# ScalarE issues the stores of the dense groups, SyncE their landings and loads, and each segment's rows are scaled one group sooner

## Chip, cores and metric

One core of a Trainium2 chip. The metric is the device time of one execution in microseconds; beside it stands one execution under the profiler, with its span from the first to the last instruction of the kernel. Engines are named as in the profile: PE (matmul), DVE (VectorE), ACT (ScalarE), POOL (GpSimd), SP (SyncE).

## What is computed

N = 16384 tokens of 256 features, each with a segment number `bids` from 0 to 7. Tokens are placed in padded segments of 3072 rows, attended within their segment, projected, normalized over all tokens and added to the input:

```python
q, k, v = feat @ Wq, feat @ Wk, feat @ Wv
starts = jnp.searchsorted(bids, jnp.arange(B))
pos = jnp.arange(N) - starts[bids]
qp, kp, vp = pad(q), pad(k), pad(v)
scores = jnp.where(mask[:, None, :], einsum(qp, kp), NEG)
r = einsum(softmax(scores), vp)[bids, pos]
t = r @ Wt
tn = (t - t.mean(0)) / jnp.sqrt(t.var(0) + EPS) * gamma + beta
return feat + jax.nn.relu(tn)
```

`bids` is not sorted. So only tokens whose `pos` lies within 3072 of zero own a row of their segment; all others read one of two edge rows of a segment.

## The kernel before

`fast_path` writes each engine's program once, in the order in which operations are added with `pg.op`; `Program.settle` works out from the boxes that an operation reads and writes which semaphores it must wait for. Each engine runs its own list in that order, so an operation that waits holds all that stand behind it on its engine.

First come eight segments of attention, up to 6 tiles of 128 rows each. Their rows lie in `tk` (line 939), the gathered inputs in `xs`. The table `order` (line 989), a list of the 16 dense groups, is computed early on DVE; SP reads its 16 entries into registers (line 1531, through `load`, line 1068: one register load and two register instructions behind it). POOL likewise reads `upto`, the count of groups that each segment needs.

Then follows the last stage. Sums over all tokens give mean and variance; the chain on DVE goes through a square root on ACT (line 1860) to `scale` and `shift`, and to the 16 edge rows in three bf16 parts (`y3`). The dense groups (loop at line 1933, NG = 16) each write 1024 tokens of the output, all as if they were edge readers: group k's input is loaded into buffer `fb[k % NF]` (NF = 10, `load_group`, line 1698), PE multiplies a one-hot table `hot` with `y3` into four PSUM banks (24 matmuls), and the sum of input and banks goes back to `fb`. `PAIRS` (line 1872) says for how many of the four banks PE also adds the input (`open_group`) so that ACT only copies the bank (line 1949); the others DVE adds (line 1952, "addition k" below). The banks of even and odd groups alternate, so PE's group k+2 needs the banks that addition k and copy k free.

All 17 stores (`store`, line 1923; group 0 in two halves) are issued by SP. After store k SP waits for the landing of store k-1 and raises `groups_done` (`finish`, line 1920), then issues load k-3+NF (line 1957). From k = 3 to 10 DVE scales, shifts and adds the rows of segment k-3 behind addition k (`normal`, line 1892: three operations over four tiles; `normal_more`, line 1904: three more for a fifth and a sixth tile, if the segment has them), at k = 11 the 3 tiles of late rows `tl`. POOL scatters these rows over the output (lines 1981 to 1998), for each segment only after enough groups have landed: the wait at line 1982. At the end each engine loads a flag and looks at it (`look`, line 1970); the landing of store 15 is waited for by SP behind its look (line 1979).

Of the kernel before, what the change touches and what calls it, by code (L numbers as in the profile page):

```python
# [21 lines left out]
NB = 8  # L22
# [878 lines left out]
def fast_path(nc, feat, bids, wq, wk, wv, wt, gamma, beta, out, bad):  # L901
# [6 lines left out]
    NG = J // GT  # L908
# [3 lines left out]
    pg = Fast(nc)  # L912
# [12 lines left out]
    def new(name, shape, dtype=F32):  # L925
        nonlocal end
        size = mybir.dt.size(dtype)
        for d in shape[1:]:
            size *= d
        plan.append((name, shape, dtype, end))  # L930
        h = at(name, shape, dtype, end)
        end += size + -size % 32
        return h
# [8 lines left out]
    vs, q, k = [None] * 2, [None] * 2, [None] * 2  # L942
# [17 lines left out]
    NF = len(fb)  # L960
# [28 lines left out]
    upto, order = new("upto", [1, NB + 1], I32), new("order", [1, NG], I32)  # L989
# [76 lines left out]
    regs = pg.sized  # L1066

    def load(eng, key, ap, hi, lo=0):
        def emit(e):
            regs[key] = e.value_load(ap, min_val=lo, max_val=hi)  # L1070

        pg.op(eng, emit, [ap], [], bare=True)
# [623 lines left out]
    GR = GT * P  # L1696

    def load_group(k):
        f = fb[k % NF]

        def emit(e):
            rows = feat[ds(regs[("order", k)] * GR, GR), :]
            return e.dma_start(f[:], rows.rearrange("(p i) d -> p i d", p=P))

        pg.op("SP", emit, [], [f[:]], dma=True)
# [129 lines left out]

    for g in range(MID, NF):
        load_group(g)
    for t in range(LT):
        pg.gather(tl[:, t, :], t_rows, ridl[:, t : t + 1], NB * FW)

# [33 lines left out]
    def open_group(k):  # L1874
        f = fb[k % NF]
        for r in range(4 - PAIRS[k], 4):
            pg.mm(
                bank[4 * ((k + 1) % 2) + r][:], ident[:], f[:, 2 * r : 2 * r + 2, :].rearrange("p t d -> p (t d)"),
                start=True, stop=False,
            )  # L1880
# [11 lines left out]
    def normal(m, T, y=tk, x=xs):  # L1892
        y, x = y[:, m : m + T, :], x[:, m : m + T, :]

        def over_t(a):
            return a.unsqueeze(1).to_broadcast([P, T, D])

        pg.tt(y, y, over_t(scale), ALU.mult)
        pg.tt(y, y, over_t(shift), ALU.add)
        pg.stt(y, y, 0.0, x, ALU.max, ALU.add)  # L1900
# [3 lines left out]
    def normal_more(e, t):  # L1904
        m = e * FT + t
        y, x, sem, n = tk[:, m, :], xs[:, m, :], row_done[e], 3 * (t - 4)

        def emit(v):
            with v.If(regs[("td", e)] > t - 4):
                v.tensor_tensor(y, y, scale, ALU.mult).then_inc(sem, 1)  # L1910
                v.wait_ge(sem, n + 1)
                v.tensor_tensor(y, y, shift, ALU.add).then_inc(sem, 1)  # L1912
                v.wait_ge(sem, n + 2)
                v.scalar_tensor_tensor(y, y, 0.0, x, ALU.max, ALU.add).then_inc(sem, 1)

        pg.op("DVE", emit, [y, x, ss[:]], [])
# [3 lines left out]
    def finish(w):  # L1920
        pg.op("SP", lambda e: e.sem_inc(done, 1), [], [], after=w)

    def store(k, lo, hi):
        f = fb[k % NF]

        def emit(e):
            rows = out[ds(regs[("order", k)] * GR, GR), :]
            return e.dma_start(rows.rearrange("(p i) d -> p i d", p=P)[:, lo:hi, :], f[:, lo:hi, :])

        return pg.op("SP", emit, [f[:, lo:hi, :]], [], dma=True)  # L1930

    stores = []
    for k in range(NG):
        f = fb[k % NF]
        b0 = 4 * ((k + 1) % 2)
        own_pairs = 4 - PAIRS[k]
        if k >= 2:
            open_group(k)
        for u in range(2):
            for part in range(3):  # L1940
                for r in range(4):
                    s = slice(32 * r, 32 * r + 2 * NB)
                    pg.mm(
                        bank[b0 + r][:, u * D : (u + 1) * D], hot[s, k, u, :], y3[part][s, :],
                        start=(r < own_pairs and part == 0), stop=(part == 2),
                    )
        if own_pairs < 4:
            rows = f[:, 2 * own_pairs : 8, :].rearrange("p t d -> p (t d)")
            pg.copy("ACT", rows, psum[:, b0 + own_pairs : b0 + 4, :].rearrange("p b d -> p (b d)"))
        for lo, hi in ((0, 2), (2, 3)) if k == 0 else ((0, own_pairs),):  # L1950
            rows = f[:, 2 * lo : 2 * hi, :].rearrange("p t d -> p (t d)")
            added = pg.tt(rows, rows, psum[:, b0 + lo : b0 + hi, :].rearrange("p b d -> p (b d)"), ALU.add)
        stores.append([store(k, 0, 4), store(k, 4, 8)] if k == 0 else [store(k, 0, 8)])
        if k >= 1:
            finish(stores[k - 1])
        if k >= 3 and k - 3 + NF < NG:
            load_group(k - 3 + NF)
        if 3 <= k < 3 + NB:
            e = k - 3
            normal(e * FT, 4)  # L1960
            normal_more(e, 4)
            normal_more(e, 5)
        if k == 3 + NB:
            normal(0, LT, tl, xl)
    again = {}

    for eng in ENGINES:
# [2 lines left out]
    def look(eng, after=()):  # L1970
        def emit(e):
            again[eng] = (e, regs[("again", eng)], e.mark_branch_hint_location())

        pg.op(eng, emit, [], [], bare=True, after=after)

    look("PE", [added])
    for eng in ("ACT", "DVE", "SP"):
        look(eng)
    finish(stores[NG - 1])

    for e in range(NB):
        pg.op("POOL", lambda x, e=e: (x.wait_ge(done, 1), x.wait_ge(done, regs[("g", e)])), [], [])
# [26 lines left out]
def whole(nc, feat, bids, wq, wk, wv, wt, gamma, beta, out):  # L2009
    with nc.sbuf_tensor("bad", [P, 1], I32) as bad:  # L2010
        ends = fast_path(nc, feat, bids, wq, wk, wv, wt, gamma, beta, out, bad)
        engines = [e for e, _, _ in ends]
        for e, again, mark in ends:
            e.br_cond(again > 0, "general", "all_done").branch_hint(mark)
        with nc.body("general", valid_engines=OrderedEngineSet([e.engine for e in engines])):
            nc.all_engine_barrier()
            with tile.TileContext(nc) as tc:
                any_lengths(tc, feat, bids, wq, wk, wv, wt, gamma, beta, out)
        nc.switch_bb("all_done")
# [34 lines left out]
```

## Time and profile before

| | us |
|---|---|
| median of 3 runs (lowest to highest) | 341.26 (341.05 to 342.02) |
| profiled execution, its own time | 340.02 |
| its span | 335.6 |
| DVE busy in the span | 238.0 (71%) |
| PE busy | 258.8 (77%) |
| POOL busy | 135.4 (40%) |
| ACT busy | 151.4 (45%) |
| last Square on ACT, and the Sqrt after it | 235.91, 242.90 |
| dense groups: first addition, last addition ends | 248.25, 329.1 |
| mean DMA rate from 254 to 302 | about 395 GB/s |

The profile counts from the first instruction. A row of a timeline gives start, duration, engine, line, operation, output<-input, and in brackets how long the engine was idle before it and what ended that. "remote" or "another core or an unknown queue" means that the profile has no instruction that matches the end of the wait. Busy time of PE and POOL is rough: PE's ends are modelled, and POOL's spans are approximate. The DMA queue q1 is SP's, q10 ACT's, q0 POOL's.

### The profile page before, as it was taken

The numbers are of one execution on the slowest core, as the hardware profiler recorded it, in microseconds if no ns is written. First come the engines' busy times: TensorE is split into PE (matmuls) and PEld (weight loads), VectorE is DVE, ScalarE is ACT, GpSimd is POOL, SyncE is SP. The second block draws the span as 40 slices with busy tenths as digits, with TensorE's granted clock in tenths as the row PEclk, the third lists the DMA queues.
The fourth block names the chain that finished last, engine by engine and source line by source line (L and its number), as shares of the span: only waits on it lengthen the run. The fifth ranks groups of instructions, "written<-read, shape, count | busy, mean of one in ns | idle before, by whom it ended". The sixth has DMA issues, their size and how long they took to land.

```text
span 335.6 us, 4870 instructions
## 1 busy us (share of the span) xinstructions
PE 258.8 (77%) x1407; PEld 169.9 (51%) x1407; DVE 238.0 (71%) x765; ACT 151.4 (45%) x294; POOL 135.4 (40%) x143
## 2 busy tenths in 40 slices
PE   5699799998998999899999979295858966455100
PEld 2466556666666777677667856164423422122000
DVE  4835679996775759478759878445589999999202
ACT  3126968767755762656476377384310311110000
POOL 6434215060350160325003647742120647887750
PEclk9999989999999999999999999769585976555555
DMA  3101004151171033203001210399969999997933
GB/s 99 33 22 47 17 3 130 41 152 37 29 169 48 0 88 115 66 9 109 31 3 47 83 32 2 114 375 389 418 267 373 315 428 420 422 413 294 373 115 131
DMA packets 21533, 52.50 MB, mean 156 GB/s; under 512 B 5488, under 2 KB 14786, under 8 KB 17530
## 3 DMA queue, kind: packets, MB, share of 16 engines
q1 hardware_dynamic: 15674, 41.37, 32.4%
q0 software_dynamic: 5280, 10.18, 10.2%
q10 hardware_dynamic: 544, 0.52, 0.5%
q8 instruction: 16, 0.26, 0.3%
q14 instruction: 19, 0.16, 0.1%
HBM read 26.27 MB, written 28.74 MB: 164 GB/s over the span
## 4 chain that ended last, share of the span: by engine, by line
PE 45%; DVE 25%; ACT 9%; issue 6%; another core or an unknown queue 6%; POOL 3%; DMA 2%; POOLq 0%; DVEq 0%
PE ps L802 43%; DVE f L821 7%; DVE tk L821 5%; ACT pa L812 4%; ACT xT L812 2%; PE ps L807 2%; DMA ecat<-t_rows,eidx 2%; ACT vs L817 2%; DVE junk L828 1%; DVE k L818 1%; POOL sel L830 1%; DVE tk L1910 1%; DVE tk L1912 1%; DVE w L821 1%
## 5 line engine op out<-in xcount | busy, mean ns | idle before, releaser
L877 POOL DMA_INDIRECT xs<-in_r_feat,idx x48 | 51.0, 1063 | 118.9 <-DVE idx L841 70.3
L802 PE MATMUL ps<-vs,pa 128*128 128x257 f32 x312 | 80.7, 404 | 10.5 <-ACT tk L812 6.0
L802 PEld LDWEIGHTS ps<-vs,pa 128*128 128x128 f32 x312 | 59.1, 198 | 24.9 <-issue 10.3
L893 POOL DMA_INDIRECT out<-tk,idx x32 | 36.6, 1144 | 28.0 <-DVE f L821 15.8
L802 PE MATMUL ps<-wvt,xT 128*128 128x256 f32 x156 | 37.4, 386 | 0.7 <-ACT vs L817 0.7
L817 ACT COPY f<-ps 128x1024 f32<-128x1024 f32 (+1 forms) x12 | 10.0, 834 | 61.4 <-remote 40.2
L802 PE MATMUL ps<-y,hot 16*128 16x256 bf16 x384 | 20.1, 356 | 22.5 <-DVE f L821 14.5
L821 DVE TENSOR_TENSOR f<-f,ps 128x1024 f32<-128x1024 f32 (+3 forms) x17 | 26.2, 1561 | 14.9 <-remote 14.2
L802 PEld LDWEIGHTS ps<-wvt,xT 128*128 128x128 f32 x156 | 28.8, 190 | 11.0 <-ACT sq L812 2.3
L812 ACT ACTIVATE pa<-ps,mask 128x512 f32<-128x512 f32 x48 | 29.5, 687 | 10.2 <-PE ps L802 9.8
L802 PEld LDWEIGHTS ps<-y,hot 16*128 16x128 bf16 x384 | 11.0, 117 | 40.3 <-DVE f L821 21.3
L802 PE MATMUL ps<-f,ident 128*128 128x512 f32 x38 | 27.7, 854 | 1.6 <-DVE f L821 0.9
L854 DVE RECIPROCAL rdens<-ps 128x1 f32<-128x1 f32 x48 | 7.7, 160 | 27.3 <-PE ps L802 23.9
L817 ACT COPY vs<-ps 128x512 f32<-128x512 f32 x24 | 14.1, 589 | 27.1 <-PE ps L802 17.3
L812 ACT ACTIVATE xT<-ps,negx 128x512 f32<-128x512 f32 (+1 forms) x32 | 16.9, 581 | 19.4 <-PE ps L807 9.8
L818 DVE COPY k<-ps 32x128 f32<-32x128 f32 x48 | 14.1, 294 | 16.0 <-PE ps L802 13.3
L802 PE MATMUL ps<-xT,w 128*128 128x512 f32 (+1 forms) x48 | 22.0, 586 | 1.5 <-ACT xT L812 1.5
L812 ACT ACTIVATE q<-ps,cqk 96x512 f32<-96x512 f32 (+3 forms) x32 | 18.3, 573 | 10.3 <-PE ps L802 10.0
L841 DVE SCALAR_TENSOR_TENSOR acc<-tk,reads_r,acc 128x256 f32<-128x256 f32 x45 | 21.4, 476 | 2.0 <-issue 1.3
L841 DVE SCALAR_TENSOR_TENSOR acc<-sq,reads_r,acc 128x256 f32<-128x256 f32 x45 | 21.7, 483 | 0.0
L812 ACT ACTIVATE pb<-ps,mask 128x256 f32<-128x256 f32 x48 | 19.2, 475 | 4.1 <-PE ps L802 3.8
L802 PE MATMUL ps<-q,k 32*128 32x512 f32 (+1 forms) x124 | 20.0, 560 | 0.0
(264 smaller groups left out, 420.9 us busy)
## 6 DMA issues: line engine op xcount, KB each, us to landing
f<-in_r_feat SPq DMA_DIRECT2D x16, 1024.0 KB, 9.8
out<-f SPq DMA_DIRECT2D x15, 1024.0 KB
t_rows<-tk SPq DMA_DIRECT2D x8, 512.0 KB, 5.8
t_rows<-tk SPq DMA_DIRECT2D x8, 256.0 KB, 3.3
eb<-edge_of SPq DMA_DIRECT2D x16, 64.0 KB
out<-f SPq DMA_DIRECT2D x2, 512.0 KB, 3.4
xs<-in_r_feat,idx POOLq DMA_INDIRECT x48, 3.1
out<-tk,idx POOLq DMA_INDIRECT x39
```

The costliest lines, as they stand in the source:

```text
L802: "PE", lambda e: e.matmul(out, lhsT, rhs, start=start, stop=stop, skip_group_check=True),
L807: return self.op("PE", lambda e: e.transpose(out, in_, ident), [in_, ident], [out], pred=pred)
L812: "ACT", lambda e: e.activation(out, in_, func, bias=bias, scale=scale), [in_, *more], [out]
L817: return self.op("ACT", lambda e: e.copy(out, in_), [in_], [out])
L818: return self.op(eng, lambda e: e.tensor_copy(out, in_), [in_], [out])
L821: return self.op(eng, lambda e: e.tensor_tensor(out, a, b, op), [a, b], [out])
L828: lambda e: e.tensor_scalar(out, a, s1, s2, op0, op1, accum_out=accum)
L830: else e.tensor_scalar(out, a, s1, s2, op0, op1),
L841: else e.scalar_tensor_tensor(out, a, s, b, op0, op1),
L854: return self.op("DVE", lambda e: e.reciprocal(out, in_), [in_], [out])
L877: lambda e: e.indirect_dma_start(out=out, out_offset=None, in_=table, in_offset=bass.IndirectOffsetOnAxis(ap=ind, axis=0), bounds_check=n ...
L893: lambda e: e.indirect_dma_start(out=table, out_offset=bass.IndirectOffsetOnAxis(ap=ind, axis=0), in_=src, in_offset=None, bounds_check=n ...
```

## The change

Four things change. ACT reads the 16 entries of `order` into registers of its own (key "at"), in its order behind the last operation of the attention and ahead of the square root. The stores are issued by ACT. The store of group k-1 is put behind ACT's copy of group k, and `finish` of that store and the load that it makes room for follow at once on SP, so loads come as soon as the store that frees their buffer has landed, instead of three groups later. And the rows of segment e are scaled behind addition e+2 instead of e+3; `tl` behind addition 10. The wait for the last landing moves ahead of SP's flag load and look.

```diff
     for g in range(MID, NF):
         load_group(g)
+    for k in range(NG):
+        load("ACT", ("at", k), order[0:1, k : k + 1], NG - 1)
     for t in range(LT):
         pg.gather(tl[:, t, :], t_rows, ridl[:, t : t + 1], NB * FW)
...
         def emit(e):
-            rows = out[ds(regs[("order", k)] * GR, GR), :]
+            rows = out[ds(regs[("at", k)] * GR, GR), :]
             return e.dma_start(rows.rearrange("(p i) d -> p i d", p=P)[:, lo:hi, :], f[:, lo:hi, :])
 
-        return pg.op("SP", emit, [f[:, lo:hi, :]], [], dma=True)
+        return pg.op("ACT", emit, [f[:, lo:hi, :]], [], dma=True)
 
     stores = []
+
+    def send(k):
+        stores.append([store(k, 0, 4), store(k, 4, 8)] if k == 0 else [store(k, 0, 8)])
+        finish(stores[k])
+        if k + NF < NG:
+            load_group(k + NF)
+
     for k in range(NG):
...
             pg.copy("ACT", rows, psum[:, b0 + own_pairs : b0 + 4, :].rearrange("p b d -> p (b d)"))
+        if k >= 1:
+            send(k - 1)
         for lo, hi in ((0, 2), (2, 3)) if k == 0 else ((0, own_pairs),):
...
-        stores.append([store(k, 0, 4), store(k, 4, 8)] if k == 0 else [store(k, 0, 8)])
-        if k >= 1:
-            finish(stores[k - 1])
-        if k >= 3 and k - 3 + NF < NG:
-            load_group(k - 3 + NF)
-        if 3 <= k < 3 + NB:
-            e = k - 3
+        if 2 <= k < 2 + NB:
+            e = k - 2
             normal(e * FT, 4)
             normal_more(e, 4)
             normal_more(e, 5)
-        if k == 3 + NB:
+        if k == 2 + NB:
             normal(0, LT, tl, xl)
+    send(NG - 1)
     again = {}
...
     for eng in ("ACT", "DVE", "SP"):
         look(eng)
-    finish(stores[NG - 1])
```

## The prediction

> **What bounds the kernel now.** I read the busy table in slices first: from about 246 us the kernel is in its last stage, the dense groups, where DVE and the DMA engines are both full. Then the chain of waits of the end:
>
> ```profile
> 306.88 1.24 DVE f L821
> 308.12 0.42 issue
> 308.55 2.28 DVE f L821
> 310.82 3.16 another core or an unknown queue
> 314.00 0.04 issue
> 314.04 1.75 DVE f L821
> 315.79 10.90 another core or an unknown queue
> 326.75 0.04 issue
> 326.79 2.29 DVE f L821
> ```
>
> The last two additions of a group (k=14, k=15) wait 3.16 and 10.90 us for something the page can't name. It isn't the load: the landing records in the trace put the last load at 298.4. What is left is PE's bank for that group, whose matmuls the trace draws as ended at 312.4. After the last addition (329.1) the store of group 15 is issued, lands at 334.8 (SP's landing record, line 1921), and the span ends at 335.6. The table by stretches shows the stage before it:
>
> ```profile
> 278.00:286.00 8.00, 5.10 (x28) 1.95 (x28) 7.80 (x12) 1.01 (x1) 6.47 (x6) 0.58 1.02 424
> 286.00:294.00 8.00, 3.51 (x30) 1.31 (x34) 7.79 (x12) 1.01 (x1) 6.17 (x7) 0.50 1.02 420
> ...
> 318.00:326.00 8.00, 0.00 (x0) 0.00 (x0) 0.00 (x0) 0.00 (x0) 5.02 (x6) 0.50 0.44 159
> ```
>
> Columns: length, busy time of PE, PE loads, DVE, ACT, POOL, clock, DMA share, GB/s. DVE is 97% busy and DMA full; at 318 to 326 POOL alone works. So I read POOL's timeline:
>
> ```profile
> 261.30 1.71 POOL L893 DMA_INDIRECT out<-tk,idx  x1 [15.17 <-DVE f L821]
> ...
> 265.91 1.83 POOL L893 DMA_INDIRECT out<-tk,idx  x1 [0.30 <-DVE f L821]
> 271.45 0.98 POOL L893 DMA_INDIRECT out<-tk,idx  x1 [3.71 <-SPq L1921]
> ```
>
> POOL's scatters of segment 1 wait for SP's landing count, not for rows: by lines 1453 to 1481 and the inputs, segments 0 to 7 need 3, 5, 5, 7, 7, 7, 11 and 11 landed groups, and the fifth landing was counted at 270.6. The rows of segment 1 were ready at 264.6. From 271.45 on POOL issues one scatter every 1.29 us or slower, without a pause, to 324.54; its drain (L789) ends at 331.9, three microseconds before the last store. POOL's chain is the second bound, close behind the first.
>
> **What the Trainium skill says.** "DMA: Bandwidth & Descriptors", section "Issuing engines are not separate DMA queues": DMAs from scalar, sync and gpsimd run on the same 16 engines, and several issuers only save issue time. The trace agrees on the size of that: 17 stores at 0.33 us of SP each, while the DMA share stands at 1.02. The same page, "Queues, rings and completion order": each DMA engine goes round-robin between the rows that have work, packet by packet. In the kernel before, stores and loads sit in one row (q1) in issue order, so its trace doesn't show it. "Perfetto Trace Analysis", "Summary: the profiler window per engine type": TensorE's end is estimated. This trace fits: drawn end 312.4, addition released at 326.75.
>
> **The change, part by part.** The profiled execution took 340.02, its span 335.6; the median of the runs is 341.26, 1.24 above it. I sum against 335.6.
>
> 1. *Sixteen register loads on ACT.* They stand in ACT's order after the last Square and ahead of the Sqrt for the scale, on which all of DVE's later work hangs:
>
> ```profile
> 235.91 0.42 ACT L812 ACTIVATE sq<-tk 128x256 f32<-128x256 f32 x1
> 236.34 1.28 ACT L812 ACT_TABLE_LOAD   x1
> 242.90 0.30 ACT L812 ACTIVATE s<-v,eps_t 128x8 f32<-128x8 f32 x1 [5.27 <-DVE v L830]
> ```
>
> SP does the same sixteen, and ACT has one load at its end (line 1070):
>
> ```profile
> L1070 SPq TENSOR_LOAD <-order x16: 265/267/489, 79.3 to 87.8; - x16
> ...
> L1070 ACTq TENSOR_LOAD <-bad x1: 1067/1067/1067, 314.1 to 314.1; - x1
> ```
>
> Each load has two register instructions behind it: on SP sixteen took 79.3 to 88.4 = 9.0 us. Started at 235.95 they end at 244.95, 2.05 past 242.90. If the table load stays next to its Sqrt, behind them, 1.28 more: D = 3.4. Lower end: 2.1, the table load ahead. Upper end: ACT's only load in the trace took 1.6 with what follows it; sixteen of those are 25.8, D = 20. That one was a first load, and SP's and POOL's first were also slower than their next (0.49 against 0.27), so I take D = 3.6, a slow first one included. Nothing hides it: DVE waits at 242.9 for the Sqrt, and PE and the loads of the first ten groups (landed by 249.6) are early.
>
> 2. *Stores from ACT.* SP loses 17 issues of 0.33, and nobody waited for them. ACT gains 17 of some 0.48 (its two issues at the start: 0.465 and 0.497). The store of k-1 waits for DVE's addition k-1 and holds what is behind it on ACT: the copy of k+1. That copy needs PE's banks of k+1, which the same addition frees, and PE takes 0.8 us or more after that: covered, so 0; without the cover 0.5 a group. The store of k-1 also waits for the copy of k, normally done earlier; for k=14 (copy at 314.06, addition 13 done 310.83) it leaves 3.2 late, covered by the store of 15 being last.
>
> 3. *Loads on SP at once after a landing.* Loads 10 to 15 were issued at 260.6, 263.4, 270.8, 276.4, 282.9, 288.7 and each landed 13 us or more before its first reader (load 10 at 266.9, PE's matmul with group 10 at 280.5; load 14 at 290.4, PE at 305.5): no gain from having them sooner. But they now share the engines with the stores from another row, instead of standing behind stores 0 to 3. This is the hidden cost, taken in 5.
>
> 4. *Rows one group sooner.* DVE's sum is the same, 98% full to 310.8; only the order moves. Additions 3 to 10 come later by one segment's rows (3.7 us for four tiles, up to 6.2 with two more). Addition 4 ended at 260.97; now additions 0 to 2 (254.0), rows 0 (3.7), addition 3 (2.3), rows 1 (3.7), addition 4 (1.2): 264.85 + D = 268.4. The rows were not what POOL waited for, so the earlier rows gain nothing, and the fifth landing gets later.
>
> 5. *POOL's start.* Before: store 4 issued 261.2, landed 270.6, behind one load. After: issued 268.5. If the engines gave it all, it would land 3.4 later (the median landing of the half store): 271.9. With loads taking half from about 258.5: stores have moved 1.8 of 5.24 MB by then (0.37 MB/us, as in this stretch before), the other 3.4 go at 0.185: 277. I take 277, between 271.9 and 279. POOL's segment 1 starts near 277.5 instead of 271.45: +6 (range +1.4 to +8). All its later gates (landing 7 near 288, landing 11 near 310, rows) are met before it gets there, so its 53.1 us follow unchanged, ending at 330.6.
>
> 6. *The last landing on SP.* The wait for landing 15 now stands ahead of SP's load of the flag, which was done while the store was under way (329.54 to 330.44). It comes after the landing now: +0.95 on the path to the end.
>
> **Sum.** DVE and store tail: D 3.6 + 0.95 = +4.5, if the 10.90 wait stays. If that wait goes with POOL's last scatter (326.7 against 324.54), 6 + 0.95 = +7. POOL's own end: 331.9 + 6 + 0.7 = 338.6, +3.0. I take +4.7, since the first needs only that the wait stays what it is: 340.02 + 4.7 + 1.24 = **346.0**; this case's own range is 344.8 to 348.6.
>
> **Rivals.**
> - *The tail wait goes away, POOL ends the kernel* (slower side, 0.20). For it: loads are out of the way at the end. Additions 14 and 15 then end at 318.8, the last store by 328, and the end is POOL's 338.6: 344.3, or 342 with a POOL start at +4.
> - *The same, with a short POOL shift: faster* (0.14). If stores aren't slowed by loads, store 4 lands at 271.9, POOL shifts by 1.4 and ends at 331.9 + 1.4 + 0.7 = 334.0, 1.6 under 335.6: 339.7. It decides where POOL's start is under 2.9 later and the 10.90 wait is gone. Against it: the wait follows PE's last group, which the diff leaves as it is.
> - *Within 0.3%* (0.08): the two effects meet, 340.2 to 342.3.
> - *ACT's loads at its own 1.6 each* (0.04): D near 20, about 362.
> - The main case has 0.54. That the change doesn't do what it says I rule out: the store's queue is in the diff.
>
> A measurement of this kernel can tell about 0.3% from no change. Faster 0.14, same 0.08, slower 0.78. The range leaves out the faster rival's lower part and the 1.6 us loads: 339.8 to 350.
>
> **What would show it.** Right: sixteen TENSOR_LOADs on ACT from about 236, the Sqrt at 246.3 to 246.6 instead of 242.90; stores on q10; addition 4 ending near 268.4; landing 5 counted near 277 and POOL's segment 1 released by it; loads 10 to 15 issued by 284; a flag load on SP after the last landing. Wrong: a Sqrt still near 243 (step 1), landing 5 at or before 271 (step 5), or the last addition following addition 13 without a wait, which would take the main case with it.

## The result and the profile after

| | before | after |
|---|---|---|
| median of the runs, same job | 341.64 (341.05 to 342.56) | 352.56 (351.95 to 353.85) |
| profiled execution, its span | 340.02, 335.6 | 353.07, 348.5 |
| Sqrt on ACT starts | 242.90 | 246.70 |
| addition 4 ends | 260.97 | 268.66 |
| fifth landing counted | 270.6 | 279.5 |
| last scatter issued | 323.56 | 331.53 |
| last landing counted | 334.8 | 346.8 |

The ratio is 1.0322, 95% interval 1.0281 to 1.0363: slower by 10.9 us, where 4.7 was forecast; 352.56 lies outside the range of 339.8 to 350. A job is one set of kernels measured together on one chip, the kernel before among them. Comparisons below are made within one job unless the text says otherwise, because the kernel before itself took 330 in some jobs and 339 to 342 in others; how these jobs differ is told with the experiments. A ratio compares only those runs of a kernel that lie within 1.5% of its fastest; a median is of all runs.

The chain of waits of the changed kernel, its end (start, length, what it was):

```profile
309.26 1.75 DVE f L821
311.06 1.61 PE ps L802 x24
312.73 1.75 DVE f L821
314.48 15.31 another core or an unknown queue
329.88 2.29 DVE f L821
332.17 3.46 another core or an unknown queue
335.69 0.85 DVE f L821
...
337.49 2.15 DVE f L821
```

Before, the two unexplained waits were 3.16 and 10.90 us and stood ahead of additions 14 and 15. Now they are 15.31 and 3.46 and stand ahead of additions 13 and 14. One group was left behind the long wait; now there are three, and their stores are issued within 4 us of one another, at 335.87, 337.61 and 339.81.

The queues show the change itself. The stores' 16.78 MB have moved from q1 to q10, where 0.52 MB of ACT's own stood before. First before, then after:

```profile
q1 hardware_dynamic: 15674, 41.37, 32.4%
q10 hardware_dynamic: 544, 0.52, 0.5%
...
q1 hardware_dynamic: 13226, 24.60, 19.2%
q10 hardware_dynamic: 2992, 17.30, 12.3%
```

ACT's timeline after, around the Sqrt and around stores 3 and 4 (start, length, idle time before in brackets):

```profile
235.57 0.42 ACT L812 ACTIVATE sq<-tk 128x256 f32<-128x256 f32 x1
245.41 1.28 ACT L812 ACT_TABLE_LOAD   x1 [9.42 <-issue]
246.70 0.30 ACT L812 ACTIVATE s<-v,eps_t 128x8 f32<-128x8 f32 x1
...
264.04 0.34 ACTq L1930 DMA_DIRECT2D out<-f  x1
269.59 1.01 ACT L817 COPY f<-ps 128x1024 f32<-128x1024 f32 x1 [5.13 <-PE ps L802]
269.81 0.34 ACTq L1930 DMA_DIRECT2D out<-f  x1
```

The 9.42 us of "issue" are the sixteen register loads; the table load stands behind them. Store 4 goes out at 269.81, although its addition ended at 268.66: copy 5, which stands ahead of it on ACT, waited for PE.

POOL's timeline after:

```profile
265.62 1.55 POOL L893 DMA_INDIRECT out<-tk,idx  x1 [20.37 <-DVE tk L821]
...
280.37 0.98 POOL L893 DMA_INDIRECT out<-tk,idx  x1 [8.43 <-SPq L1923]
...
331.53 0.98 POOL L893 DMA_INDIRECT out<-tl,idx  x1 [0.30 <-issue]
```

Segment 1 again waits for SP's count of landings, now for 8.43 us, and starts 8.9 later than before.

PE's timeline after shows what the chain can't name:

```profile
306.88 1.47 PE L802 MATMUL ps<-y,hot 16*128 16x256 bf16 x24
311.06 1.47 PE L802 MATMUL ps<-y,hot 16*128 16x256 bf16 x24 [2.70 <-DVE f L821]
...
317.00 0.38 PE L802 MATMUL ps<-y,hot 16*128 16x256 bf16 x1 [0.34 <-issue]
318.41 0.41 PE L802 MATMUL ps<-y,hot 16*128 16x256 bf16 x2 [1.03 <-issue]
319.84 0.43 PE L802 MATMUL ps<-y,hot 16*128 16x256 bf16 x3 [1.01 <-issue]
```

Group 13's 24 matmuls are drawn from 311.06 as if they took 1.47 us, but group 14's weight loads and matmuls then enter in steps of 0.71 us (in the single records 316.99, 317.71, 318.41, 319.14, 319.84), as they would behind work that goes at that pace. PE's semaphore, on which the additions wait, tells the real ends: group 12 done at 312.67, group 13 at 329.79, 0.09 us ahead of addition 13. That is 17.1 us, or 24 x 0.71. I call this the crawl. Before, PE's semaphore for group 15 came at 326.70, 14.4 us after its drawn end: the same thing, one group at the end. The pace isn't the same everywhere: before, group 15 was done 12.7 us after group 14, which is 0.53 us for each matmul.

### The profile page after: what moved, and what is told of

Same layout as the page of the kernel before. It is cut to its first block, busy times and chain, and to the rows that moved or that the text cites. A ratio compares the mean times of both kernels' runs of the same rounds, so it can differ in the third digit from the quotient of the medians.

```text
span 348.5 us, 4934 instructions
## 1 busy us (share of the span) xinstructions
PE 264.0 (76%) x1407; PEld 170.1 (49%) x1407; DVE 237.9 (68%) x765; ACT 151.5 (43%) x294; POOL 134.9 (39%) x143
## 3 DMA queue, kind: packets, MB, share of 16 engines
q10 hardware_dynamic: 2992, 17.30, 12.3%
## 4 chain that ended last, share of the span: by engine, by line
PE 40%; DVE 25%; ACT 10%; another core or an unknown queue 8%; issue 7%; POOL 3%; ACTq 2%; DMA 2%; DVEq 0%; POOLq 0%
PE ps L802 38%; DVE f L821 7%; DVE tk L821 5%; ACT pa L812 3%; ACTq L1070 2%; PE ps L807 2%; ACT xT L812 2%; DMA ecat<-t_rows,eidx 2%; ACT vs L817 2%; DVE junk L828 1%; DVE k L818 1%; POOL sel L830 1%; DVE tk L1912 1%; DVE tk L1914 1%
## 5 line engine op out<-in xcount | busy, mean ns | idle before, releaser
L802 PE MATMUL ps<-vs,pa 128*128 128x257 f32 x312 | 81.0, 405 | 10.7 <-ACT vs L817 5.7
L802 PE MATMUL ps<-y,hot 16*128 16x256 bf16 x384 | 25.3, 373 | 37.5 <-DVE f L821 17.0
L802 PEld LDWEIGHTS ps<-y,hot 16*128 16x128 bf16 x384 | 12.1, 119 | 60.1 <-issue 25.3
L812 ACT ACTIVATE pa<-ps,mask 128x512 f32<-128x512 f32 x48 | 29.5, 688 | 11.6 <-PE ps L802 9.8
L802 PE MATMUL ps<-f,ident 128*128 128x512 f32 x38 | 29.3, 902 | 4.1 <-ACT f L817 1.6
L802 PE MATMUL ps<-xT,w 128*128 128x512 f32 (+1 forms) x48 | 21.2, 567 | 0.2 <-ACT xT L812 0.2
```

The costliest lines, as they stand in the source:

```text
L802: "PE", lambda e: e.matmul(out, lhsT, rhs, start=start, stop=stop, skip_group_check=True),
L812: "ACT", lambda e: e.activation(out, in_, func, bias=bias, scale=scale), [in_, *more], [out]
```

## The experiments

My theory after the result had two parts. First, TensorE's small matmuls crawl while GpSimd works through its scatters. Second, the crawl's end hangs on the scatters' chain and so on the fifth landing. The rivals were the stores' traffic, TensorE's clock, and the loads that share the engines with the stores.

**The scatters left out**, of both kernels, so that the selected rows keep their dense value. The edit, with the same for `put_now` and for the late rows `tl`:

```diff
-            pg.put(out, idx[:, m : m + 1], tk[:, m, :], N)
+            pass
```

The expectations say 39 scatters; with the three of the late rows there are 42, all left out.

> The changed kernel with the 39 indirect scatters of its last loop left out (the selected rows keep their dense value, so that part of the output is missing); GpSimd's waits, the stores, the loads and TensorE's work stay. Theory 1 (while GpSimd issues scatters and VectorE is idle, TensorE's 16-row matmuls take about 0.71 us each, so one group of 24 takes 17 us): the 15.3 us wait ahead of addition 13 falls under 2 us, the last addition ends near 319, and the time is near 331 us (328 to 335). Rival (the wait comes from the stores' traffic or from TensorE's low clock): the wait stays over 10 us and the time stays within 4 us of 352.

> The kernel before with the same scatters left out (the selected rows' final values are missing). Theory 1: the 10.90 us wait ahead of addition 15 goes, the last addition ends near 315, the time is near 326 us (323 to 330), and the distance to the changed kernel without scatters is 4 to 5 us, that is D and the flag load, not 11. Rival: the wait stays, the time is 338 to 342.

Measured: 331.86 (328.2 to 334.2) and 329.01 (328.5 to 329.09), beside 341.67 for the kernel before; ratios 0.9734 (0.9649 to 0.9819) and 0.9624 (0.9555 to 0.9694). The second is 3 over the 326 expected, still in its range; its last landing was counted at 323.7. DVE's end in the changed kernel without scatters:

```profile
304.11 5.68 DVE L821 TENSOR_TENSOR f<-f,ps 128x1536 f32<-128x1536 f32 x3
310.90 3.95 DVE L821 TENSOR_TENSOR f<-f,ps 128x1536 f32<-128x1536 f32 x2 [1.11 <-PE ps L802]
```

The first line is additions 11 to 13, the second 14 and 15, and the only wait is 1.11 us. PE's semaphores for groups 14 and 15 come at 310.84 and 312.10: 24 matmuls in 1.26 us, not 17. The stores, the loads and the granted clock (0.50 from 300 to 312 in both) are still there, so none of these makes the crawl by itself. In this job the two kernels with scatters, below, had it. So the scatters are needed for the crawl of the dense groups. The distance between the two kernels shrinks from 10.9 to 2.9 by medians, where 4 to 5 was expected; the first one's runs differ by up to 6 us.

**Part 4 alone**, in the kernel before:

```diff
-        if 3 <= k < 3 + NB:
-            e = k - 3
+        if 2 <= k < 2 + NB:
+            e = k - 2
...
-        if k == 3 + NB:
+        if k == 2 + NB:
```

> The kernel before with part 4 alone: each segment's rows scaled one dense group sooner, stores and loads still on SyncE as before. Theory 1 (with the rows done sooner only additions are left at the end, so TensorE's stall falls on group 13 with three groups behind it): 346 us (343 to 349), a wait over 10 us ahead of addition 13 or 14. Rival (the loss comes from the register loads and from the loads that share the engines with the stores): 340 to 342, the wait stays at addition 15.

Measured: 345.71 beside 341.67, ratio 1.0121 (1.0048 to 1.0194). The chain of waits of this kernel, its end:

```profile
304.81 1.75 DVE f L821
306.61 5.83 PE ps L802 x42
312.53 2.29 DVE f L821
314.82 14.69 another core or an unknown queue
329.57 0.30 DVE f L821
```

The long wait has moved from addition 15 to 14, with the stores and loads as before. My reading, which no run tests alone: with the rows gone from between the last additions, DVE runs out of work sooner, and PE has one group more to do inside the crawl.

**The register loads out of the way**, in the changed kernel: three behind the Sqrt, each other one ahead of a store.

```diff
-    for k in range(NG):
-        load("ACT", ("at", k), order[0:1, k : k + 1], NG - 1)
...
     pg.act(s8[:], v8[:], AF.Sqrt, bias=eps_t[:])
+    for k in range(3):
+        load("ACT", ("at", k), order[0:1, k : k + 1], NG - 1)
...
     def send(k):
+        if k + 3 < NG:
+            load("ACT", ("at", k + 3), order[0:1, k + 3 : k + 4], NG - 1)
```

> The changed kernel with ScalarE's register loads behind the Sqrt (three) and one ahead of each store (the other thirteen), so that the Sqrt is no later than before. Theory 1: the 3.8 us of D come back whole, 348.8 us (347.5 to 350), the stall ahead of addition 13 stays 12 us or more. Rival (the end is set by the fifth landing, which the loads' traffic holds, so D is hidden): within 1 us of the changed kernel.

Measured: 347.77 (344.56 to 350.77) beside 341.67, ratio 1.0128 (1.0015 to 1.0241). That is 4.8 less than the changed kernel had in the first job, where the kernel before took the same (341.64); the runs are spread over 6 us. It agrees with D being paid in full, and the Sqrt is back at 243.50. The wait ahead of addition 13 was only 1.9 here, and 7.8 and 10.4 ahead of 14 and 15. The crawl is there, but the same matmuls meet it later, so its place is not fixed to a group; my "12 us or more ahead of 13" was wrong.

**The loads' distance, and which quantity of the scatters counts.** Three kernels, one job. First the scatters' width: all 42 write 64 columns to a scratch table `thin`, so the selected rows' final values are missing (the same edit in `put_now` and for `tl`).

```diff
-            pg.put(out, idx[:, m : m + 1], tk[:, m, :], N)
+            pg.put(thin, idx[:, m : m + 1], tk[:, m, 0:64], N)
```

> The changed kernel with its 39 scatters writing only the first 64 of a row's 256 columns, to a scratch table (the selected rows' final values are missing from the output): as many GpSimd instructions and as many rows, a quarter of the bytes. Theory 1a (what slows TensorE is GpSimd's working through the scatters): the wait ahead of addition 13 stays over 11 us, the time is 347 to 353. Theory 1b (it is the scatters' bytes): the wait falls to a quarter, under 5 us, the time to about 337 (333 to 341).

Then the number of small matmuls:

```diff
-            for part in range(3):
+            for part in range(2):
...
-                        start=(r < own_pairs and part == 0), stop=(part == 2),
+                        start=(r < own_pairs and part == 0), stop=(part == 1),
```

> The changed kernel with the third of the three bf16 parts of y left out of the dense additions (the output loses some of its precision): 16 small matmuls in a group in place of 24. Theory 1 (a pace of 0.71 us for each small matmul while the scatters are worked through): group 13 is done 16 x 0.71 = 11.4 us after group 12, not 17.2, addition 13 starts near 324, and as TensorE gets on to group 14 earlier while the crawl's end stays where the scatters put it (near 335), the time falls by 3 to 6 us, to 347 to 350. Rival (a wait of fixed length or end, whatever is queued): addition 13 stays near 330, the time within 1.5 us of 352.6.

Then the loads' distance, on top of the register loads later:

```diff
-        if k + NF < NG:
-            load_group(k + NF)
+        if k >= 2 and k - 2 + NF < NG:
+            load_group(k - 2 + NF)
```

> loads_later_after with the loads of groups 10 to 15 put back to where they were, two landings later on SyncE. If the loads beside the stores are what holds the fifth landing: it is counted at 273 or before (276.55 in loads_later_after), GpSimd's last scatter and the crawl end about 3 us sooner, the time is 344 to 346. If not: the fifth landing stays past 275, the time within 1 us of 347.8.

Measured: 338.70, 337.83 and 334.62, ratios 1.0275 (1.0204 to 1.0345), 1.0249 (1.0184 to 1.0313) and 1.0146 (1.0083 to 1.0209), beside 330.28 for the kernel before. None of the three shows any crawl: no wait over 1.2 us ahead of additions 11 to 15. A job without the crawl tells nothing on its cause, so the first two expectations were not put to the test. The job shows what bounds the kernel without the crawl. The end of the chain of waits of the kernel with two parts:

```profile
321.01 0.98 POOL out L893
322.30 0.99 POOL out L893
323.59 0.98 POOL out L893
```

The span ends at 332.9, 8.3 us after the last scatter's instruction ended (324.57), while the last addition had ended at 311.2. GpSimd's chain of scatters sets the end, and the fifth landing starts it: from that landing to the span's end it is 61.4 to 63.1 us in the eight traces without the crawl and with the rows at k - 3 or k - 2, except one kernel told at the end. A quarter of the bytes doesn't shorten it (61.4 to 61.7 with thin scatters).

**Does the crawl belong to the chip?**

> The changed kernel once more, since the last four kernels ran where the kernel before took 330 us and showed no crawl of TensorE at all. If the crawl belongs to the chip that a kernel lands on: with the kernel before at 341 the time is 352 to 353 and a wait of 15 us stands ahead of addition 13; with the kernel before at 330 no wait over 2 us stands in the dense stage, GpSimd's chain of scatters sets the end, and the time is 339 us (338 to 340.5), the distance 8 to 9 us in place of 11. If it belongs to the kernel: a wait over 10 us wherever it runs.

> The kernel before, to have its trace from the same chip as the others of this call. With its time at 330: no wait over 2 us ahead of additions 13 to 15, the last landing well ahead of GpSimd's end, the last scatter issued near 316. With its time at 341: the wait of 10.9 us at addition 15 again.

> Part 4 alone in the kernel before, once more. Where TensorE crawls: 4 us over the kernel before, as in rows_sooner_before. Where it doesn't, the additions' place at the end no longer counts and only the later fifth landing does: 1 to 3 us over the kernel before.

Measured: 350.91, 340.19 (one run) and 344.49, beside 338.64 (332.26 to 339.97) for the kernel before in the same job; the ratios are 1.046 (1.037 to 1.0549) and 1.0264 (1.0176 to 1.0353), by medians the distances are 12.3 and 5.9 us. The crawl is back: 6.3 and 12.4 us ahead of additions 14 and 15 in the changed kernel, 4.6 and 9.6 in the kernel before, 16.1 ahead of 14 with the rows sooner. So the expectation for a job with the crawl held roughly in time (12.3 over the kernel before, where 11 to 12 was expected), not in the wait's place. A later job on a chip of the same number had none, so the chip's number doesn't decide it. What does stays open.

The attention stage tells at once which kind a job is: DVE's first quotient of segment 7 starts at 220.2 to 222 in the traces with the crawl and at 206.5 to 212.3 in those without (216.0 in the changed kernel without scatters, whose whole front ran some 4.5 us earlier). It also shows that TensorE crawls there without any scatter. ACT copies the product of the last segment's matmuls out of PSUM; in the ten traces with the crawl, the two kernels without scatters among them, this copy starts 3.5 to 5.1 us after the drawn end of these matmuls, in the ten others 0.5 us after it. In the kernel before, PE's and POOL's timelines, and then the chain of waits, where the lateness is again a wait that the profile can't name:

```profile
206.64 3.91 PE L802 MATMUL ps<-wvt,xT 128*128 128x256 f32 x16
209.07 1.21 POOL L877 DMA_INDIRECT reads_r<-reads_of,idx  x1 [0.30 <-issue]
...
211.14 4.34 another core or an unknown queue
215.48 0.57 ACT vs L817
```

Again GpSimd works through indirect transfers, here gathers from 201.23 to 216.92, up to 213.33 of only 4 bytes a row; the granted clock was 1.00 from 206 to 212. This speaks for GpSimd's instructions, and against the bytes and the clock. But no run tests it, and the same gathers run without harm in the other jobs. It divides the difference between the jobs, too: where no register loads stand ahead of it, the Sqrt starts at 242.1 to 244.1 with the crawl and at 235.7 to 236.5 without. So about 7 of the 10 us that the kernel before differs by are lost ahead of the dense groups.

**The crawl's cause, and the stores alone.** The last is the kernel before with `store` on ACT, its loads of registers as in the kernel with the register loads later, landings and the loads at their old distance on SP; rows as before.

> thin_scatter once more (a quarter of the scatters' bytes, to a scratch table; the selected rows' final values are missing), read only where TensorE crawls, which its attention stage shows (the last segment's first quotient after 218 us on VectorE, against 211 where it doesn't). Theory 1a (GpSimd's working through the scatters): waits over 10 us in sum ahead of additions 13 to 15, 348 to 353 us. Theory 1b (their bytes): under 5 us in sum, 341 or less.

> two_parts once more (the third bf16 part of y left out: less precise output, 16 small matmuls in a group), read where TensorE crawls. With a pace of 0.71 us for each small matmul: a group that lies whole in the crawl takes 11.4 us, and the time falls by 3 to 6 us against the changed kernel's 351 to 352.5. With a fixed end of the crawl that all queued work waits for: within 1.5 us.

> loads_old_distance once more (the changed kernel with ScalarE's register loads behind the Sqrt and the loads of groups 10 to 15 at their old distance). Where TensorE crawls: the fifth landing near 272, against 276.5 in loads_later_after, and 344 to 346 us against its 347.8; without effect of the loads: 347 to 348.5.

> The kernel before with its stores issued by ScalarE alone (register loads behind the Sqrt and ahead of each store, group 15's landing counted ahead of the flag load as in the change): rows and loads where they were. By the prediction's steps 2 and 6: 0 to 1 us over the kernel before. If the stores' own queue lets loads and stores share the engines differently: 2 us or more over it, with a later fifth landing.

Measured beside 330.36 (330.04 to 330.76): 338.77, 338.34, 334.85 and 334.05; ratios 1.026 (1.0242 to 1.0277), 1.0235 (1.0218 to 1.0252), 1.013 (1.0113 to 1.0147), 1.0117 (1.0088 to 1.0145). Again no crawl, so the first two stay without a verdict. But these narrow intervals give the change's parts: stores on ACT +3.7, then rows sooner +0.8, then the register loads ahead of the Sqrt and the loads at once some +3.5 to 3.9, as far as two kernels that leave work out stand for the whole change. I had forecast 0 to 1 for the stores. ACT's timeline of the kernel with the stores alone shows a part of it:

```profile
251.70 1.01 ACT L817 COPY f<-ps 128x1024 f32<-128x1024 f32 x1 [8.70 <-PE ps L802]
252.47 0.34 ACTq L1930 DMA_DIRECT2D out<-f  x1
254.38 1.01 ACT L817 COPY f<-ps 128x1024 f32<-128x1024 f32 x1 [1.67 <-PE ps L802]
255.74 0.34 ACTq L1930 DMA_DIRECT2D out<-f  x1
```

Addition 3 had ended at 249.10 and addition 4 at 253.88. Their stores go out 3.4 and 1.9 us later, each behind the copy of the group after, which waits for PE, and behind a register load that stands ahead of each store in this kernel and not in the changed one: 0.6 us of the 3.4 and 1.1 of the 1.9. On SP it was 1.9 and 0.2. From its issue store 4 then takes 10.7 us to its landing, against 9.4. Measured from the start of the Sqrt, to take D and the front of each job out, the fifth landing comes after

| | us after the Sqrt | traces |
|---|---|---|
| kernel before | 27.7, 27.7 | 2 |
| rows sooner alone | 29.5, 29.7 | 2 |
| stores on ACT alone | 30.7 | 1 |
| stores on ACT, rows sooner, loads at the old distance | 32.4, 33.0 | 2 |
| the same, loads at once (D removed) | 33.0 | 1 |
| the whole change | 32.8, 33.3 | 2 |

Rows and stores add up, 1.9 and 3.0. Loads at once add nothing over loads at the old distance. That doesn't clear the loads: at the old distance, too, those of groups 10 and 11 run beside store 4 (issued at 253.89 and 258.43, the store at 258.03), and 2.0 MB move on q1 in the store's 10.5 us. The last kernel below shows what the store takes without them.

**A third try at the scatters' bytes**

> thin_scatter a third time (a quarter of the scatters' bytes, to a scratch table; the selected rows' final values are missing), to be read for the crawl only where the kernel before takes 336 us or more. Theory 1a (GpSimd's working through the scatters): waits over 8 us in sum ahead of additions 13 to 15, 348 us or more. Theory 1b (their bytes): under 4 us in sum, 345 or less. Where the kernel before takes 330: 338.8 us again.

Two runs, 333.83 and 339.24, beside 330.63: no crawl in the trace. Instructions or bytes stays open for the dense groups.

**Versions.** If the rows' place matters, later rows might help; if the fifth landing matters, so should keeping loads away from store 4:

```diff
-        if 3 <= k < 3 + NB:
-            e = k - 3
+        if 6 <= k < 6 + NB:
+            e = k - 6
...
-        if k == 3 + NB:
+        if k == 6 + NB:
```

> The kernel before with each segment's rows scaled three dense groups later (at k - 6, the ninth set at 14): VectorE has rows to do between the last additions, and those come forward. Theory 1 (TensorE crawls only where the scatters go on beside a VectorE that waits): the last groups' matmuls are done before VectorE runs dry, the last landing comes under 325, and GpSimd's chain of scatters (1.29 us each, from the rows' new times) sets the end: 337 us (334 to 341). Rival (the rows come too late for the scatters, which then end later than 324.5): 344 us or more.

Measured: 333.02 beside 330.28, ratio 1.0087 (1.0028 to 1.0147). There was no crawl to remove in that job, and now the rows are what the scatters wait for: segment 1's first came 32.1 us after the Sqrt, where the kernel before has 28.5. The fifth landing came at 27.8, where the kernel before has 27.7, and it is no longer what sets the end: 64.6 us from it to the end. With the crawl it was not tried.

```diff
-        if k >= 3 and k - 3 + NF < NG:
-            load_group(k - 3 + NF)
+        if k >= 5 and k - 5 + NF < NG:
+            load_group(k - 5 + NF)
```

> The kernel before with the loads of groups 10 to 15 two landings later still (at k - 5), so that none shares the engines with the store of group 4. If loads hold the fifth landing: it comes 1.5 to 2.5 us sooner, GpSimd's chain with it, and the time falls by 1.5 to 2 us. If not, or if a load is then late for its addition: no gain, or a loss of 1 us and more.

> loads_two_later_before on another chip. If the end is the fifth landing plus GpSimd's chain: 1.5 to 3 us under the kernel before where TensorE doesn't crawl, 2 to 4 us under it where it does. If the first chip's result was chance: within 0.3%.

Measured: in the first job 335.94 (14 runs) beside 338.64, 2.7 less by medians, but the ratio is 1.0025 (0.9976 to 1.0073): a gain is not shown. In the second 329.63 (22 runs) beside 330.63, 1.0 less by medians, ratio 0.9926 (0.9898 to 0.9954): faster by 0.7%. The fifth landing came 23.2 us after the Sqrt in place of 27.7: with no load beside it, store 4 landed 5.2 us after its issue, in both jobs, against 9.4 and 9.6. So in one row, too, it is loads that hold the fifth landing. Segment 1 then starts 3.5 us sooner after the Sqrt than in the kernel before of the first job. The last scatter goes out only 1.6 sooner. Of the 1.9 us lost on the way, 1.1 are a wait for the eleventh landing, which is late now (counted at 308.54, against 305.23):

```profile
309.39 0.98 POOL L893 DMA_INDIRECT out<-tk,idx  x1 [1.06 <-SPq L1921]
```

It is the best version I have, beside both kernels.

## Why the forecast was right in its sign and wrong in its size

**Step 1, right.** D was taken as 3.6; the Sqrt moved by 3.8, the table load stood behind the loads, and D came back when the loads were moved. Sixteen loads took 235.59 to 245.37, 9.8 us; the first three were dearer, where the text counted on one:

```profile
L1070 ACTq TENSOR_LOAD <-order x16: 273/275/784, 235.6 to 244.9; - x16
```

**Step 2, wrong.** "Covered, so 0": the store of k-1 was said to wait for a copy of k that is "normally done earlier". For k-1 = 4 it isn't, and the store waits 0.95 us behind copy 5; in the kernel with the stores alone both store 3 and store 4 wait. The step also left out what the stores' own row does to their transfers, which stands in step 5. Together the stores on ACT cost 3.0 us up to the fifth landing, the register loads ahead of each store included, and 3.7 in the whole.

**Steps 3 and 5, right in the chain, short in size.** The fifth landing was taken at 277 and came at 279.51; POOL's start moved by 8.9, over the top of "+1.4 to +8". Addition 4 was right: 268.66 against 268.4. Of the missing 2.5 us, 1.3 are in store 4's issue (269.81, where 268.5 was taken) and 1.2 in its transfer (9.70 us, where 8.5 was taken). The low end was too low: it took the 3.4 us of a half store, and a whole one without loads beside it takes 5.2. The sharing between two rows, taken from the Trainium skill ("DMA: Bandwidth & Descriptors", "Queues, rings and completion order"), fits the traces, though no run tests it alone. Store 3 took 11.1 us to its landing, against 4.7 before, and 1.2 MB of loads moved on q1 while store 4 was under way. With the rows sooner alone, in one row, store 4 lands 7.3 and 7.8 us after its issue; in all kernels with the stores on ACT it takes 9.7 to 11.3. By the table of landings the 8.9 us are D 3.8, rows 1.9 and stores on ACT some 3.

**Step 6, right.** The last landing was counted at 346.8 and the span ended 1.7 later, against 0.8: +0.9.

**The sum, where the forecast failed.** The step is "I take +4.7, since the first needs only that the wait stays what it is". The wait didn't stay: the one of 10.90 ahead of addition 15 became 15.31 and 3.46 ahead of additions 13 and 14. The text held it fixed because it "follows PE's last group, which the diff leaves as it is"; but those groups are slow by the crawl, which in the dense groups needs the scatters, and more of them met it now. The text had weighed "if that wait goes with POOL's last scatter ... +7" and left it; with +7 it would have been 348.3, still 4.3 short. PE's last slow group was done at 326.70 before and at 335.60 after; the last scatter was issued at 323.56 and 331.53. Over seven traces with the crawl (both kernels twice, rows sooner twice, the register loads later) the crawl ends 3.1 to 4.1 us after the last scatter's issue. In an eighth, with the loads two later, group 15 was done at 322.2, just as the last scatter went out. So that the crawl's end hangs on the scatters' end is likely, but not shown. In the spans of the two pairs of traces the sum is not D and the flag but

| term | first job | second pair |
|---|---|---|
| end of the crawl (326.70 to 335.60, 326.71 to 336.55) | +8.9 | +9.8 |
| from there to the last landing (8.1 to 11.2, 8.1 to 8.9) | +3.1 | +0.8 |
| flag load | +0.9 | +0.9 |
| span (335.6 to 348.5, 335.6 to 347.1) | +12.9 | +11.5 |

The second term is large where two more stores stand behind the last long wait, as in the first job. From the Sqrt to the end the changed kernel takes 101.8 and 100.3 us with the crawl, and the two kernels nearest to it 93.4 to 94.7 without. The kernel before takes 92.7 and 92.4 with the crawl; without, it has no trace, and by an estimate, from its spans of 325.5 to 326.2 and the Sqrt at 235.7 in the kernels with the same front, about 90. So the crawl of the dense groups costs the kernel before some 2.5 us and the changed one 6 to 8. In the first job the profiled runs differ by 13.1, the medians by 10.9, since the profiled run of before lay 1.6 under its median and that of after 0.5 over.

The rival "the tail wait goes away, POOL ends the kernel" describes the jobs without the crawl. Its faster form needed a start of POOL under 2.9 us later; parts of the change alone exceed that. The whole change was not run in such a job; the two kernels nearest to it, with thin scatters and with two parts, stood 7.6 to 8.4 us over the kernel before.

## What to carry to other kernels

When a chain of waits names "an unknown queue" for 10 us, find out what ends that wait before you assume that it stays: compare the drawn ends of the producer with its semaphore, see which other engine works through it, and take that engine's work out to test it. A store that moves to an engine with work of its own is issued behind that work, and it matters first where another engine counts the landing. A gate on a count of landings hands every delay of one landing to all that follows it.

## What the runs showed of the hardware

A matmul of 16 rows by 256 columns took about 0.71 us in the changed kernel while GpSimd's scatters went on and DVE waited (0.53 in the kernel before), and 0.05 us (24 in 1.26 us, over four banks) without scatters. The Trainium skill's "TensorE: Matmul & The Clock Gate", section "What's actually happening", has a cold clock of 1.2 GHz, which by an estimate is 0.21 us for 256 columns: the clock gate alone doesn't give 0.71, and the granted clock was 0.50 with the crawl and without it. In the same jobs TensorE was 3.5 to 5.1 us late in the attention stage, beside GpSimd's gathers, at a granted clock of 1.00. Whole jobs show the crawl and others don't; the kernel before differs by some 10 us between them, about 7 of it ahead of the dense groups. GpSimd's scatters went out every 1.29 us, and a quarter of the bytes left their chain as long. After the last scatter's instruction the span went on for 8.3 us, in which GpSimd drained.
